# Layer 1 edges: a PSUM bank of VectorE's own for node numbers, group weights, directions and kv factors, and two banks of node sums

## The chip, the cores and the metric

The kernel runs on one core of a Trainium2 chip. A core has five engines, each with a queue of its own: TensorE (PE, matrix products, with the weight loads shown apart as PEld), VectorE (DVE), ScalarE (ACT), GpSimd (POOL) and SyncE (SP, which here only issues DMAs). Two memories lie on the core: SBUF, and PSUM with eight banks of 512 float32 a partition, into which TensorE writes its products. [...] The metric is the time of one execution on the device in microseconds (us), as the median of several runs.

## What is computed

The reference is a graph network of two layers on 3125 nodes with 256 features and 50,000 edges sorted by their target node. What matters here is the first part of layer 1: an attention over edges (`gnn`) and a linear attention over all nodes (`mix`), both on the normed nodes:

```python
# gnn: 64 features a message, 4 heads
h_fwd = h @ W_forward.T
h_rev = h @ W_reverse.T
messages = h_fwd[src] * direction[:, 0:1] + h_rev[src] * direction[:, 1:2]
scores = leaky_relu(einsum('ef,hf->eh', messages, attn_forward[0]), 0.2)
exp_scores = exp(scores - scores.max(axis=0))
sum_exp = segment_sum(exp_scores, dst, N)
norm = exp_scores / (sum_exp[dst] + 1e-10)
out[:, hd] = segment_sum(messages * norm[:, hd:hd + 1], dst, N)      # for each head

# mix: 8 heads of 64
q, k, v = heads of einsum('bnc,fc->bnf', x, Wqkv)
k, v = inst_norm(k), inst_norm(v)
out = einsum('bhnd,bhde->bhne', q, einsum('bhnd,bhne->bhde', k, v)) / n
out = einsum('bnf,cf->bnc', heads joined, Wout) + bout
```

After it follows a feed-forward part with four experts and a second edge attention that picks the experts.

## The kernel before

`layer1_mix` (L1530) does both parts in one loop. The 50,000 edges are laid out as 391 columns of 128, and `SPANS` cuts the columns into 50 groups: one of 4, 48 of 8, one of 3. For each group:

- `fetch` (L1562) issues one row gather for each column on POOL's queue (`gather`, L69): 128 rows of 136 numbers from the table `tab1` in DRAM, picked by a column of `t_src`, into a tile `g1` of which four exist. The gathers of three groups are issued ahead, and those of group i+3 in turn i of the loop.
- `messages` (L1569) makes the group's messages on VectorE. L1573 and L1575 multiply the two halves of the gathered rows by the edge's two directions `t_dir`, L1577 adds them, L1579 forms the scores, L1584 their maximum on each partition. TensorE turns that maximum (L1586).
- `weigh` (L1623), for the group before, multiplies the messages by the four exponents (L1624, 128x2048).
- `maximum` (L1589) keeps the running maximum of all scores: L1593 to L1595 on VectorE, with two more small transposes (L1599) on TensorE.
- `products` (L1627), for the group before, sums the weighted messages by node: matrix products (L1630) of the weighted messages with a matrix of zeros and ones, into a PSUM tile `pw`, of which three exist, a bank each.
- `add` (L1634), for two groups back, adds the sums into `acc`: L1638 and L1639 on VectorE, L1642 and L1640 on ScalarE.
- `ones_of` (L1612) makes the matrix of zeros and ones for the group: L1617 compares each edge's target `t_dst` with the node numbers of the group's window. The numbers lie in `turned` for even groups and in the first 128 columns of `self.node` for odd ones.
- `exponents` (L1602) subtracts the maximum (L1605) and lets ScalarE take the exponents (L1607) straight into the last column of the tile `v`.

A generator, `galerkin` (L1683), runs the linear attention in between: one step of it after most turns of the loop. In the steps for the 25 node tiles, VectorE sums the squares of keys and values (L1712), and multiplies the values by one factor a head (`kv_both`, L1713 to L1718), while TensorE makes keys and values (L274, from `token_matmul`) and their products (L1721). The last seven steps multiply out the result (L1776, L1778) and add it to `x` (L1769).

The loop stands under a manual schedule: TensorE, VectorE and ScalarE do their instructions in the order in which the program writes them. POOL does the gathers in its own order, SP the loads of weights. The PSUM is shared out in full: two banks for `ln_pt` (L1537), one for `pdots`, three for `pw` (L1539), two for `psm`.

Of the kernel before, what the change touches and what calls it, by code (L numbers as in the profile page):

```python
# [9 lines left out]
F32 = mybir.dt.float32  # L10
# [7 lines left out]
PSUM = bass.MemoryType.PSUM  # L18
# [4 lines left out]
P = 128  # L23
# [7 lines left out]
GROUP = 8  # L31
# [63 lines left out]
def held(t):  # L95

    return P if t < NT - 1 else REST
# [31 lines left out]
class Kernel:  # L129
# [1400 lines left out]
    def layer1_mix(self, acc):  # L1530
        nc, tc, a = self.nc, self.tc, self.a
        W, HD = 68, 64
        with ExitStack() as m:
            big = m.enter_context(tc.tile_pool(name="l1", bufs=1))
            wk = m.enter_context(tc.tile_pool(name="l1w", bufs=2))
            gp = m.enter_context(tc.tile_pool(name="l1g", bufs=3))
            ps_a = m.enter_context(tc.tile_pool(name="l1pa", bufs=2, space=PSUM))  # L1537
            ps_c = m.enter_context(tc.tile_pool(name="l1pc", bufs=1, space=PSUM))
            ps_w = m.enter_context(tc.tile_pool(name="l1pw", bufs=3, space=PSUM))  # L1539
            ps_s = m.enter_context(tc.tile_pool(name="l1ps", bufs=2, space=PSUM))  # L1540

            xT, tab1 = self.xT, self.tab1
# [5 lines left out]
            turned = big.tile([128, P], F32, name="turned")  # L1548
            for s, base in ((slice(0, HALF), HALF), (slice(HALF, P), 0)):
                nc.gpsimd.iota(turned[:, s], pattern=[[1, HALF]], base=base, channel_multiplier=0,  # L1550
                               allow_small_or_imprecise_dtypes=True)


            unit = big.tile([P, NT, 4], F32, name="unit")
            top = big.tile([4, 1], F32, name="top0")
# [6 lines left out]
            def fetch(i):  # L1562
                j0, n = SPANS[i]
                g = gp.tile([128, GROUP, 2 * W], F32, name="g1", bufs=4)
                for k in range(n):
                    gather(nc, g[:, k, :], tab1[:], self.t_src[:, j0 + k:j0 + k + 1])
                return g

            def messages(i, g):  # L1569

                j0, n = SPANS[i]
                o = gp.tile([128, GROUP, W], F32, name="msg1")
                nc.vector.tensor_mul(o[:, :n, :], g[:, :n, :W],  # L1573
                                     self.t_dir[:, j0:j0 + n, 0:1].to_broadcast([128, n, W]))
                nc.vector.tensor_mul(g[:, :n, W:], g[:, :n, W:],  # L1575
                                     self.t_dir[:, j0:j0 + n, 1:2].to_broadcast([128, n, W]))
                nc.vector.tensor_add(o[:, :n, :], o[:, :n, :], g[:, :n, W:])  # L1577
                s = gp.tile([128, GROUP, 4], F32, name="score1")
                nc.vector.scalar_tensor_tensor(s[:, :n, :], o[:, :n, HD:], 0.2, o[:, :n, HD:],  # L1579
                                               op0=OP.mult, op1=OP.max)  # L1580
                if j0 + n == NJ:
                    nc.vector.tensor_scalar(s[:, n - 1, :], s[:, n - 1, :], late, None, op0=OP.add)
                mx = gp.tile([128, 4], F32, name="mx1")
                nc.vector.tensor_reduce(mx, s[:, :n, :].rearrange("p j h -> p h j"), AX.X, OP.max)  # L1584
                pt = ps_s.tile([4, 128], F32, name="psm")
                nc.tensor.transpose(pt, mx, self.ident)  # L1586
                return o, s, pt

            def maximum(pt):  # L1589

                nonlocal top
                two = gp.tile([4, 3], F32, name="top")
                nc.vector.tensor_reduce(two[:, 2:3], pt, AX.X, OP.max)  # L1593
                nc.vector.tensor_tensor(two[:, 0:1], two[:, 2:3], top, OP.max)
                nc.vector.tensor_sub(two[:, 1:2], top, two[:, 0:1])  # L1595
                top = two[:, 0:1]
                pb = ps_s.tile([128, 2, 4], F32, name="psm")
                for i in range(2):
                    nc.tensor.transpose(pb[:, i, :], two[:, i:i + 1].to_broadcast([4, 128]), self.ident[:4, :4])  # L1599
                return pb  # L1600
# [11 lines left out]
            def ones_of(i):  # L1612

                j0, n = SPANS[i]
                hot = gp.tile([128, GROUP, P], F32, name="hot")
                iota = turned if i % 2 == 0 else self.node[:, :P]
                nc.vector.scalar_tensor_tensor(  # L1617
                    hot[:, :n, :], self.t_dst[:, j0:j0 + n, None].to_broadcast([128, n, P]),
                    float(HALF * (1 - i)), iota[:, None, :].to_broadcast([128, n, P]),
                    op0=OP.add, op1=OP.is_equal)  # L1620
                return hot

            def weigh(n, o, v):  # L1623
                nc.vector.tensor_mul(v[:, :n, :, :HD], o[:, :n, None, :HD].to_broadcast([128, n, 4, HD]),  # L1624
                                     v[:, :n, :, HD:].to_broadcast([128, n, 4, HD]))

            def products(n, v, hot):  # L1627
                pw = ps_w.tile([P, 4, HD + 1], F32, name="pw")
# [15 lines left out]
                    nc.scalar.copy(unit[p, t, :], big2[p, 0, :])  # L1644

            with tc.manual_schedule(engines={ET.PE, ET.DVE, ET.Activation}):
                todo = self.galerkin(big, wk, ps_a, ps_c, xT)
                S = len(SPANS)
                ahead = [fetch(i) for i in range(3)]
                msg, exps, summed = {}, {}, {}  # L1650
                for i in range(S + 2):
                    if i + 3 < S:
                        ahead.append(fetch(i + 3))
                    if i < S:
                        n = SPANS[i][1]
                        o, s, pt = messages(i, ahead[i])
                    if 0 <= i - 1 < S:
                        weigh(SPANS[i - 1][1], msg[i - 1][0], exps[i - 1][2])
                    if i < S:
                        pb = maximum(pt)  # L1660
                    if 0 <= i - 1 < S:
                        summed[i - 1] = products(SPANS[i - 1][1], exps[i - 1][2], msg[i - 1][1])
                    if 0 <= i - 2 < S:
                        add(i - 2, *exps[i - 2][:2], summed[i - 2])
                    if i < S:
                        msg[i] = o, ones_of(i)
                        exps[i] = exponents(n, s, pb)
                    if i % 4 != 3 or i > 34:
                        next(todo, None)
                last = exps[S - 1][0]  # L1670
                for _ in todo:
                    pass
# [7 lines left out]
            nc.vector.reciprocal(den, den)  # L1680
            nc.vector.tensor_mul(den, den, unit)

    def galerkin(self, big, wk, ps_a, ps_c, xT):  # L1683

        nc, a = self.nc, self.a
# [20 lines left out]
        for t in range(NT + 1):  # L1708
            if t > 0:
                kv, sq = kvs.pop(t - 1)  # L1710
                var = wk.tile([P, 16], F32, name="kv_var")
                nc.vector.tensor_reduce(var, sq, AX.X, OP.add)  # L1712
                nc.vector.tensor_scalar(var, var, 1.0 / 64, LN_EPS, op0=OP.mult, op1=OP.add)  # L1713
                both = wk.tile([P, 8], F32, name="kv_both")
                nc.vector.tensor_mul(both, var[:, 0:8], var[:, 8:16])
                nc.scalar.activation(both, both, AF.Sqrt)
                nc.vector.reciprocal(both, both)
                nc.vector.tensor_mul(kv[:, 8:, :], kv[:, 8:, :], both[:, :, None].to_broadcast([P, 8, 64]))  # L1718
                for hp in range(4):
                    p = held(t - 1)  # L1720
                    nc.tensor.matmul(pc[:, hp, :],  # L1721
                                     kv[:p, 8 + 2 * hp:10 + 2 * hp, :].rearrange("p a b -> p (a b)"),
                                     kv[:p, 2 * hp:2 * hp + 2, :].rearrange("p a b -> p (a b)"),
                                     start=(t == 1 and hp == 0), stop=(t == NT and hp == 3),
                                     skip_group_check=True)
            if t < NT:
                kv = wk.tile([P, 16, 64], F32, name="kv")
                for i in range(2):
                    pk = ps_a.tile([P, 512], F32, name="ln_pt")
                    self.token_matmul(pk, xT, t, wkv[:, :, 512 * i:512 * i + 512])  # L1730
                    nc.scalar.copy(kv[:, 8 * i:8 * i + 8, :].rearrange("p a b -> p (a b)"), pk)
                sq = wk.tile([P, 16, 64], F32, name="kv_sq", bufs=1)
                nc.scalar.activation(sq, kv, AF.Square)
                kvs[t] = kv, sq
            yield
# [22 lines left out]
        g = big.tile([128, 2, D], F32, name="gm")  # L1758
# [8 lines left out]
        for t0 in range(0, NT + 4, 4):  # L1767
# [3 lines left out]
            for t in range(t0, min(NT, t0 + 4), 2):  # L1771
                m = min(2, NT - t)
# [701 lines left out]
```

## Time and profile before

| | |
|---|---|
| median of 9 runs | 2994.75 us (2976.45 to 3017.75) |
| the profiled execution | 2987.9 us, span 2986.2 us |
| busy in the span: PE, DVE, ACT, POOL | 2138.5, 1468.0, 823.3, 1641.4 us |
| gathers of layer 1's edges (L69, into `g1`), first start to last start | 1739.4 to 2328.0 us |
| first and last L1573 (messages) start | 1746.3 and 2334.7 us |
| in 1800 to 1900 us: PE, DVE, ACT, POOL busy | 69.67, 75.29, 39.38, 79.89 us |
| in 2200 to 2330 us: PE, DVE, ACT, POOL busy | 104.97, 85.08, 11.23, 103.61 us |
| L1624, 128x2048, x50 | 112.5 us, mean 2249 ns |
| L1617, 128x1024, x25 with `turned`, x25 with `node` | 30.1 and 29.6 us, mean 1205 and 1183 ns |
| L1573, L1575, L1577, x50 each | 35.6, 35.2, 35.6 us |
| L1718, 128x512, x25 | 17.3 us, mean 692 ns |

The table is read so: the profile is of one execution, taken by the hardware, with the start and the duration of each instruction. "Busy" counts the time in which an engine works on an instruction, so a share well below the whole can still belong to the engine that sets the pace, if the rest of its time are gaps that belong to its work. In lists of groups, "idle before" is the time that the engine stood still just before these instructions, with what ended it; "issue" means that nothing in the profile was waited for. A gather's row is the time in which POOL handles it, not the transfer, which lands later.

### The profile page before, as it was taken

Reading aid. Unit: us, or ns where it says so; the run is one execution under the profiler, and the core shown is the slowest. Engines: PE = TensorE matmul, PEld = TensorE weight load, DVE = VectorE, ACT = ScalarE, POOL = GpSimd, SP = SyncE. Lnnn points to the kernel's source line nnn. Section 1 sums busy time; section 2 is a strip of 40 time slices with the busy share of each in tenths; the row PEclk is TensorE's granted clock in tenths of the full one; section 3 lists DMA queues with packets and bytes.
Section 4 is the critical chain, followed back from the end, with each engine's and each line's share of the span. In section 5 each row is a group of like instructions: output and inputs, shape, how many; then the busy total and the mean of one; then the engine's idle time right before and its main releaser. Section 6 shows DMA issues by size and latency. Waiting matters only on the chain.

```text
span 2986.2 us, 26612 instructions
## 1 busy us (share of the span) xinstructions
PE 2138.5 (72%) x8219; PEld 1479.8 (50%) x8219; DVE 1468.0 (49%) x3847; ACT 823.3 (28%) x1789; POOL 1641.4 (55%) x1931
## 2 busy tenths in 40 slices
PE   1455688278989699898999456676777566877935
PEld 0233344134555377787778334444455444545623
DVE  7258947366733493111111447777766711112345
ACT  1143133325522112223223223333410321212213
POOL 5858867680000803666664057787887376666220
PEclk9677699589968899999999678888888687988967
DMA  8312438021100214555554322222222111112123
GB/s 274 131 46 92 155 141 289 1 78 49 61 1 28 98 55 128 171 165 177 160 180 152 104 68 47 47 46 46 46 53 46 31 33 14 16 25 59 46 76 90
DMA packets 191716, 263.27 MB, mean 88 GB/s; under 512 B 57234, under 2 KB 152071, under 8 KB 191563
## 3 DMA queue, kind: packets, MB, share of 16 engines
q1 hardware_dynamic: 137551, 211.02, 21.4%
q0 software_dynamic: 48864, 45.64, 7.3%
q10 hardware_dynamic: 5148, 4.80, 0.5%
q8 instruction: 67, 1.10, 0.2%
q14 instruction: 86, 0.70, 0.1%
HBM read 180.80 MB, written 80.55 MB: 88 GB/s over the span
## 4 chain that ended last, share of the span: by engine, by line
PE 37%; issue 18%; DVE 14%; POOL 13%; another core or an unknown queue 9%; ACT 5%; DMA 3%; SPq 0%; ACTq 0%; DVEq 0%; POOLq 0%
POOL g L69 11%; PE pb L1138 6%; PE fph L1853 6%; PE fpy L1869 5%; PE pb L573 4%; PE pc L1147 4%; PE pb L274 2%; PE pc L573 2%; PE pc L956 2%; PE pb L616 1%; POOL adj L76 1%; PE pb L943 1%; DVE s_z L1362 1%; PE pc L1378 1%
## 5 line engine op out<-in xcount | busy, mean ns | idle before, releaser
L69 POOL DMA_INDIRECT g<-tab,t_src x391 | 471.1, 1205 | 201.4 <-issue 199.3
L76 POOL DMA_INDIRECT adj<-ch_sum,ch_place x391 | 408.3, 1044 | 174.1 <-issue 64.3
L76 POOL DMA_INDIRECT sorted<-src,pos x256 | 245.1, 958 | 170.4 <-DVE pos L1401 92.5
L69 POOL DMA_INDIRECT G<-tabg,g_src x256 | 250.9, 980 | 131.3 <-issue 73.0
L1138 PE MATMUL pb<-xs,w 128*128 128x256 f32 x1024 | 246.4, 397 | 42.8 <-ACT h L1140 41.3
L1853 PE MATMUL fph<-xT,fw 128*128 128x512 f32 (+2 forms) x448 | 193.1, 580 | 69.3 <-ACT fh L1855 41.0
L1138 PEld LDWEIGHTS pb<-xs,w 128*128 128x128 f32 x1024 | 201.1, 199 | 83.0 <-ACT h L1140 50.6
L1630 PE MATMUL pw<-v,hot 128*128 128x260 f32 x782 | 231.9, 461 | 0.0
L1147 PE MATMUL pc<-w,h 128*128 128x256 f32 x1024 | 226.1, 379 | 0.0
L1869 PE MATMUL fpy<-fw,fh 128*128 128x256 f32 (+1 forms) x800 | 185.5, 390 | 33.4 <-issue 33.2
L573 PE MATMUL pb<-adj,sup 128*128 128x448 f32 (+1 forms) x484 | 196.8, 552 | 15.6 <-DVE r_tot L1249 13.9
L1147 PEld LDWEIGHTS pc<-w,h 128*128 128x128 f32 x1024 | 192.2, 190 | 24.9
L1140 ACT ACTIVATE h<-pb,b 128x256 f32<-128x256 f32 x256 | 116.1, 473 | 316.4 <-issue 244.3
L1630 PEld LDWEIGHTS pw<-v,hot 128*128 128x128 f32 x782 | 177.4, 233 | 35.0
L1869 PEld LDWEIGHTS fpy<-fw,fh 128*128 128x128 f32 (+1 forms) x800 | 154.8, 195 | 69.5 <-issue 44.5
L1360 ACT ACTIVATE s_z<-s_y,s_val 128x128 f16<-128x128 f16 x256 | 112.4, 486 | 199.4 <-issue 190.4
L1853 PEld LDWEIGHTS fph<-xT,fw 128*128 128x128 f32 x448 | 89.1, 203 | 155.1 <-issue 86.4
L1855 ACT ACTIVATE fh<-fph,cols 128x512 f32<-128x512 f32 (+2 forms) x112 | 68.9, 632 | 344.4 <-remote 167.1
L1150 DVE SCALAR_TENSOR_TENSOR yo<-pc,own,bg 128x256 f32<-128x256 f32 x64 | 29.0, 481 | 235.0 <-PE pb L1138 170.7
L76 POOL DMA_INDIRECT slots<-rows,abi x50 | 52.3, 1047 | 164.3 <-DVE which L1061 154.7
L573 PEld LDWEIGHTS pb<-adj,sup 128*128 128x128 f32 x484 | 90.5, 194 | 93.0 <-issue 86.5
L76 POOL DMA_INDIRECT y<-yo,toi x64 | 61.4, 959 | 132.2 <-DVE yo L1150 119.0
(570 smaller groups left out, 3808.5 us busy)
## 6 DMA issues: line engine op xcount, KB each, us to landing
adj<-zero SPq DMA_DIRECT2D x25, 1600.0 KB
w<-in_L_ffn_W1p_dram SPq DMA_DIRECT2D x32, 1024.0 KB
w<-in_L_ffn_W2p_dram SPq DMA_DIRECT2D x32, 1024.0 KB
adj<-adj SPq DMA_DIRECT2D x24, 896.0 KB
adj<-adj SPq DMA_DIRECT2D x24, 704.0 KB
slots<-empty SPq DMA_DIRECT2D x1, 8448.0 KB
srow<-slots SPq DMA_DIRECT2D x32, 264.0 KB
adj<-ch_sum,ch_place POOLq DMA_INDIRECT x391
```

Source lines behind the costliest of these rows:

```text
L69: return nc.gpsimd.indirect_dma_start(out=out, out_offset=None, in_=table, in_offset=bass.IndirectOffsetOnAxis(ap=idx, axis=0))
L76: return nc.gpsimd.indirect_dma_start(out=table, out_offset=bass.IndirectOffsetOnAxis(ap=idx, axis=0), in_=rows, in_offset=None, **kw)
L274: self.nc.tensor.matmul(out, xT[:, k, t * P:(t + 1) * P], w[:, k, :], start=(k == 0), stop=(k == 1))
L573: nc.tensor.matmul(pm[:, :w], sup[:, b, k * 128:(k + 1) * 128], mats[b, h][:, c0 - PARTS[h][0]:c0 - PARTS[h][0] + w], start=(b == b0), sto ...
L1138: nc.tensor.matmul(ph, w1[:, k, f * 128:(f + 1) * 128], xs[:, k, :], start=(k == 0), stop=(k == 1))
L1140: nc.scalar.activation(h[:, f, :], ph, AF.Gelu, bias=b1[:, f:f + 1])
L1147: nc.tensor.matmul(py, h[:, f, i * 128:(i + 1) * 128], w2[:, f, :], start=(f == 0), stop=(f == FC - 1))
L1360: nc.scalar.activation(z[:, i, k, :], y, AF.Relu, bias=val[:, k, s], scale=val[:, 2 + k, s])
L1630: nc.tensor.matmul(pw.rearrange("p h c -> p (h c)"), hot[:, k, :], v[:, k, :, :].rearrange("p h c -> p (h c)"), start=(k == 0), stop=(k == ...
L1853: nc.tensor.matmul(ph[:, :m], w1[:, k, f * 128:(f + 1) * 128], xT[:, k, t0 * P:t0 * P + m], start=(k == 0), stop=(k == 1))
L1855: nc.scalar.activation(hs[:, f, :m], ph[:, :m], AF.Gelu, bias=self.col("L1_ffn_b1", ei * FC + f))
L1869: nc.tensor.matmul(py[:p], hs[:, f, i * P:i * P + p], w2[:, f, :], start=(f == 0), stop=(f == FC - 1))
```

## The change

One of the three banks of `pw` becomes a bank of VectorE's own, `own` (128x512). Before the loop, VectorE copies the two rows of node numbers into its first 256 columns. Three small areas behind them hold a group's weights (`weight`, 8 columns of edges x 4 heads), a group's directions (`sides`, 8 x 2), and the eight factors of the values (`scales`). In each turn VectorE copies the group's directions from `t_dir` into `sides` ahead of L1573, and the exponents from the last column of `v` into `weight` ahead of L1624; these two instructions and L1575 then take their second operand from the bank. L1617 takes the node numbers from there, and the reciprocal L1717 writes its result there, from where L1718 reads it. What is computed stays the same.

```diff
-            ps_w = m.enter_context(tc.tile_pool(name="l1pw", bufs=3, space=PSUM))
+            ps_w = m.enter_context(tc.tile_pool(name="l1pw", bufs=2, space=PSUM))
+            ps_d = m.enter_context(tc.tile_pool(name="l1pd", bufs=1, space=PSUM))
...
+            own = ps_d.tile([128, 512], F32, name="own_bank")
+            nc.vector.tensor_copy(own[:, 0:P], turned)
+            nc.vector.tensor_copy(own[:, P:2 * P], self.node[:, :P])
+            weight = own[:, 2 * P:2 * P + 4 * GROUP].rearrange("p (j h) -> p j h", h=4)
+            sides = own[:, 2 * P + 64:2 * P + 64 + 2 * GROUP].rearrange("p (j i) -> p j i", i=2)
...
-                nc.vector.tensor_mul(o[:, :n, :], g[:, :n, :W],
-                                     self.t_dir[:, j0:j0 + n, 0:1].to_broadcast([128, n, W]))
-                nc.vector.tensor_mul(g[:, :n, W:], g[:, :n, W:],
-                                     self.t_dir[:, j0:j0 + n, 1:2].to_broadcast([128, n, W]))
+                nc.vector.tensor_copy(sides[:, :n, :], self.t_dir[:, j0:j0 + n, :])
+                nc.vector.tensor_mul(o[:, :n, :], g[:, :n, :W], sides[:, :n, 0:1].to_broadcast([128, n, W]))
+                nc.vector.tensor_mul(g[:, :n, W:], g[:, :n, W:], sides[:, :n, 1:2].to_broadcast([128, n, W]))
...
-                iota = turned if i % 2 == 0 else self.node[:, :P]
+                iota = own[:, i % 2 * P:i % 2 * P + P]
...
             def weigh(n, o, v):
+                nc.vector.tensor_copy(weight[:, :n, :], v[:, :n, :, HD])
                 nc.vector.tensor_mul(v[:, :n, :, :HD], o[:, :n, None, :HD].to_broadcast([128, n, 4, HD]),
-                                     v[:, :n, :, HD:].to_broadcast([128, n, 4, HD]))
+                                     weight[:, :n, :, None].to_broadcast([128, n, 4, HD]))
...
-                todo = self.galerkin(big, wk, ps_a, ps_c, xT)
+                todo = self.galerkin(big, wk, ps_a, ps_c, xT, own[:, 2 * P + 96:2 * P + 104])
...
-    def galerkin(self, big, wk, ps_a, ps_c, xT):
+    def galerkin(self, big, wk, ps_a, ps_c, xT, scales=None):
...
-                nc.vector.reciprocal(both, both)
-                nc.vector.tensor_mul(kv[:, 8:, :], kv[:, 8:, :], both[:, :, None].to_broadcast([P, 8, 64]))
+                inverse = both if scales is None else scales
+                nc.vector.reciprocal(inverse, both)
+                nc.vector.tensor_mul(kv[:, 8:, :], kv[:, 8:, :], inverse[:, :, None].to_broadcast([P, 8, 64]))
```

## The prediction

> **What bounds the kernel now.** I read the chain of waits first, then the costliest groups, then the answer for the gather's line, and last the order of time inside the stage. The chain's dearest single line and the dearest group are the same one, the row gather of the layer 1 edges:
>
> ```profile
> POOL g L69 11%; PE pb L1138 6%; PE fph L1853 6%; PE fpy L1869 5%; PE pb L573 4%; PE pc L1147 4%; PE pb L274 2%; PE pc L573 2%; PE pc L956 2%; PE pb L616 1%; POOL adj L76 1%; PE pb L943 1%; DVE s_z L1362 1%; PE pc L1378 1%
> L69 POOL DMA_INDIRECT g<-tab,t_src x391 | 471.1, 1205 | 201.4 <-issue 199.3
> ```
>
> The gather's own answer gives its spread and who waits for it:
>
> ```profile
> L69 POOL DMA_INDIRECT g<-tab,t_src x391: 940/945/3025, 1739.4 to 2328.0; - x196
> ...
>   DVE msg L1573: 92.7, 36
> ```
>
> The median is 945 ns but the mean is 1205: a quarter of a microsecond too much, 391 times. Gaps between gathers are 0.30 us throughout (119 us summed over the stage), so an undisturbed gather costs 0.945 + 0.30 = 1.25 us and 391 of them 489 us. The stretch lasts 1739.4 to 2329.4, 590 us. The 101 us between are 153 gathers of 1 us or more (the other 238 are undisturbed). The order of time shows what stretches them (start, duration, engine):
>
> ```profile
> 2008.33 0.69 DVE L1718 TENSOR_TENSOR kv<-kv,kv_both 128x512 f32<-128x512 f32 x1
> ...
> 2010.74 0.73 DVE L1573 TENSOR_TENSOR msg<-g,t_dir 128x544 f32<-128x544 f32 x1 [1.72 <-DMA g<-tab,t_src]
> 2011.38 0.72 DVE L1575 TENSOR_TENSOR g<-g,t_dir 128x544 f32<-128x544 f32 x1
> 2011.57 1.35 POOL L69 DMA_INDIRECT g<-tab,t_src  x1 [0.30 <-issue]
> ...
> 2013.25 2.30 DVE L1624 TENSOR_TENSOR v<-msg,v 128x2048 f32<-128x2048 f32 x1
> 2013.57 0.27 PE L1586 MATMUL psm<-ident,mx 128*4 128x128 f32 x1
> 2014.47 1.89 POOL L69 DMA_INDIRECT g<-tab,t_src  x1 [0.30 <-issue]
> 2015.47 0.27 DVE L1593 TENSOR_REDUCE top<-psm 4x1 f32<-4x128 f32 x1
> ...
> 2016.60 0.43 DVE L1639 TENSOR_TENSOR acc<-acc,pw 64x260 f32<-64x260 f32 x1
> 2016.67 0.94 POOL L69 DMA_INDIRECT g<-tab,t_src  x1 [0.30 <-issue]
> 2017.06 1.22 DVE L1617 SCALAR_TENSOR_TENSOR hot<-t_dst,turned 128x1024 f32<-128x1024 f32 x1
> 2017.92 1.18 POOL L69 DMA_INDIRECT g<-tab,t_src  x1 [0.30 <-issue]
> ```
>
> Each long gather ends 0.81 to 0.83 us after a VectorE instruction: 2016.36 after 2015.55 (L1624), 2012.92 after 2012.10 (L1575), 2019.10 after 2018.28 (L1617). Sorted so, the 101 us belong to L1624 46.4, L1617 30.6, L1575 with L1573 17.4, L1718 3.6, one L1703 2.1, L1577 0.9, L1638 0.8. All of these read two operands from SBUF. None ends at L1639, L1769 (one operand in PSUM) or L1712 (one operand). The close pair is L1638 and L1639, equal in size: seven gathers that start 0.02 to 0.27 us into L1638 are all held to its end. Of 32 that start so into L1639, 17 run free, like the one at 2016.67 (0.94); the other 15 are held, but to the end of L1617, which follows closely.
>
> VectorE is the second limit. From the first L1573 (1746.3) to the last (2334.7) it takes 588.4 us, of which 82.6 are waits for gathers (92.9 in the stage, less 10.35 at the first). Its own pace, with its waits for TensorE and ScalarE, is 505.8 us, above the 489 of free gathers. So the stage can fall at most about 83 us, and what the change adds to VectorE comes off that.
>
> **The change, part by part.** *Taken off the gathers.* L1573, L1575, L1617, L1624 and L1718 each get one operand in PSUM. By the sort this frees 46.4 + 30.6 + 17.4 + 3.6 = 98 us of stall. L1577, L1638 and a few small ones stay; shifted against the gathers they may catch more than their 1.7 us. A gather every 1.25 us that starts at random in 0.72 (L1577) or 0.41 (L1638) loses 0.72²/2/1.25 + 0.41²/2/1.25 = 0.27 us a group, 13 us in 49. Gathers then need 489 + 13 = 502 us, still under VectorE's pace, so this is covered.
>
> [...]
>
> *Added to VectorE.* Two copies a group: `sides` (128x16) and `weight` (128x32).
>
> ```profile
> L1713 DVE TENSOR_SCALAR kv_var<-kv_var x25: 174/174/176, 1779.4 to 2165.2; 128x16 f32<-128x16 f32 x25
> ...
> L1639 DVE TENSOR_TENSOR acc<-acc,pw x49: 416/419/429, 1786.9 to 2344.8; 64x260 f32<-64x260 f32 x49
> ...
> L1638 DVE TENSOR_TENSOR acc<-acc,grown x49: 409/422/428, 1786.5 to 2344.3; 64x260 f32<-64x260 f32 x49
> ```
>
> An instruction that doesn't need its predecessor starts 0.08 before that one's end (L1573 to L1575), one that does starts 0.04 after it (L1577 to L1579). So `sides` costs 0.17 + 0.04 = 0.21 and `weight` 0.19 (as L1579 and L1605, 32 elements) + 0.04 = 0.23. No row shows VectorE writing PSUM or reading back what it just wrote there. Low end: nothing, where VectorE waits anyway. High end: each as L1638, 0.42 + 0.12 = 0.54. Nearest in size are the 16 and 32 element rows; I take 0.27 each, 0.54 a group, the excess for the unseen PSUM write. In seven groups (36 and 38 to 43) VectorE waits 2.8 to 8.1 us for TensorE at L1593 or L1754 and the copies vanish there; 42 of the 49 periods pay: 42 x 0.54 = 22.7 us (low 0, high 42 x 1.08 = 45).
>
> *A PSUM operand in place of an SBUF one.* L1639 against L1638: 419 and 422 ns. L1769 reads 128x512 from PSUM in 672 ns, L1718 takes 691 from SBUF. I take 0. That a word is read again and again by a broadcast from PSUM is in no row; its upper price is the slower rival.
> [...]
>
> *Costs of nothing, with their cover.* The reciprocal L1717 only writes elsewhere. The two copies that fill the bank (0.30 each, as L1216's 128x136 copy) fall before the first message, where VectorE idles 10.35 us; uncovered, 0.6. `weight` waits for the exponent of the group before (L1607), done some 6 us earlier; only at the last group, where L1624 waits 0.29 now, does it stand behind it. With two banks of sums, L1630 waits for ScalarE's copy L1642 of two groups back, a period old (7 us or more). No DMA and nothing on SP's or POOL's queue moves; POOL's gathers will wait for a free `g1` buffer, that is for L1577 four groups back, some 20 us in all, which costs nothing because VectorE is then the bound.
>
> *Where the stall goes.* When VectorE no longer waits for gathers, TensorE could be late for L1593: after L1718 ends (2009.02) it needs to 2013.84, 4.8 us; VectorE needs 4.65 + 0.54 = 5.2 over the same stretch. Just covered.
>
> **Sum.** Stage 588.4 becomes 505.8 + 22.7 = 528.5, 60 us less. Everything after hangs on the stage's end. The profiled execution took 2987.9 (span 2986.2), so 2928 for it; the median of the runs is 2994.75, 6.9 above, and 2994.75 - 60 gives **2935**. Own range: copies at nothing, 2912; copies at 0.54, 2957.
>
> **Rivals.**
> *Lengthened copies.* Each write into PSUM and read back costs as much as 0.54 or somewhat more: 505.8 + 45 to 60, gain 23 to 38, time 2957 to 2972. For it: no row of such a pair. Against it: every tiny VectorE row is under 0.25. Chance 0.12.
> *The hold isn't removed.* A gather stalls for these ops wherever their second operand lies. Then the gathers still set 590 us, the copies hide in the 82.6 us of waits, and the time stays at 2995, within 5. For it: L1617 and L1624 are longer than any PSUM row here. Against it: the 17 free gathers in L1639. Chance 0.05.
> *Slower: repeated PSUM reads at half rate.* If a broadcast operand from PSUM took two cycles an element, L1624, L1617, L1573, L1575 and half an L1718 would add 2.13 + 1.07 + 0.57 + 0.57 + 0.27 = 4.6 us a group, 42 x 4.6 = 193, and the stage would be 505.8 + 22.7 + 193 = 721, 133 longer: 3128. It decides from 60/42 = 1.4 us a group, that is a third slower. For it: contiguous reads are all that the rows show. Against it: SBUF broadcasts run at full rate (L1624, 2.30 us for 2048). Chance 0.11.
>
> **How the numbers follow.** Forecast 0.72, the three rivals 0.12, 0.05 and 0.11. A measurement tells about 0.5% (15 us) from no change. Faster takes the forecast and the first rival, 0.84; the second is the same, 0.05; slower 0.11. The runs before spread by 0.7% either way, so I widen the own range by 4 below and take in most of the first rival above: 2908 to 2968.
>
> **What would show it.** The gather's mean falls from 1205 to below 1000 ns, with no long one ending 0.82 after L1624, L1617, L1575 or L1718; L1573's wait for gathers falls from 92.7 to under 20 us; POOL begins to wait for L1577; L1624 stays at 2.30 and L1617 at 1.2; the new copies read 0.17 to 0.30. A longer L1624, or a gather mean still above 1150, would prove me wrong.

## The result and the profile after

The changed kernel takes 3060.2 us (median of 20 runs, 3016.9 to 3076.5) against 2992.6 for the kernel before (62 runs): ratio 1.020, interval 1.017 to 1.023. It is about 2% slower, where 2935 was forecast. Its profiled span is 3037.0 us. Every ratio here is of fast executions alone, those within 1.5% of the fastest of their kernel, so it can differ from the quotient of the medians of all (1.023 here), and the traces of e4 and e6 below are of executions just outside that bound.

The page of the changed kernel, with the chain of waits by engine and by line, and the row of the gathers:

```profile
PE 41%; DVE 21%; another core or an unknown queue 15%; issue 14%; ACT 6%; DMA 2%; POOL 1%; ACTq 0%; DVEq 0%; SPq 0%; POOLq 0%
PE pb L1138 7%; PE pb L573 6%; PE fph L1859 5%; PE fpy L1875 5%; PE pc L1147 4%; DVE v L1629 2%; PE pc L573 2%; PE pc L956 2%; PE pb L274 1%; PE pc L1378 1%; PE pb L616 1%; ACT L1721 1%; DVE hot L1621 1%; PE pb L943 1%
...
L69 POOL DMA_INDIRECT g<-tab,t_src x391 | 372.2, 952 | 355.2 <-issue 202.1
```

The gather's mean fell from 1205 to 952 ns, and its line has left the chain. The holds are gone, as forecast. But the stage from the first message to the last (now L1579, 1724.8 to 2389.9) takes 665.1 us instead of 588.4. The chain has 15% of "another core or an unknown queue", although the program runs on one core: that share is time in which an engine waited for a semaphore and no instruction in the profile ended when it rose. The list of waits of the changed kernel (total, times, longest) says who waited so; "remote" is the same thing there:

```profile
ACT kv L1737 <- remote: 173.8, 11, 19.9
POOL g L69 <- DVE score L1583: 148.7, 21, 13.8
...
DVE top L1597 <- remote: 104.3, 11, 13.5
```

VectorE's row for L1597 shows 155.1 us idle in front of it, 104.3 of "remote" and 29.1 of "issue" among it. 665.1 less these two is 531.7, and 528.5 was forecast: these stalls account for the whole loss. The order of time shows one of them (start, duration, engine):

```profile
2030.80 3.17 PE L274 MATMUL ln_pt<-wkv,xT 128*128 128x512 f32 x7
...
2031.33 2.29 DVE L1629 TENSOR_TENSOR v<-msg,own_bank 128x2048 f32<-128x2048 f32 x1
...
2033.80 0.27 PE L1590 MATMUL psm<-ident,mx 128*4 128x128 f32 x1
2034.56 0.94 POOL L69 DMA_INDIRECT g<-tab,t_src  x1 [0.30 <-issue]
...
2040.80 0.94 POOL L69 DMA_INDIRECT g<-tab,t_src  x1 [0.30 <-issue]
2045.65 1.07 ACT L1737 COPY kv<-ln_pt 128x512 f32<-128x512 f32 x2 [18.46 <-remote]
2045.75 0.28 DVE L1597 TENSOR_REDUCE top<-psm 4x1 f32<-4x128 f32 x1 [12.13 <-remote]
```

TensorE is done with L1590 at 2034.07. ScalarE and VectorE go on only at 2045.65 and 2045.75. The trace also records when each semaphore rises: those of the two halves of L274 (ended 2032.25 and 2033.96) and of L1590 rose at 2045.63, 2045.69 and 2045.72. Elsewhere such a rise follows the end of its product by 0.01 to 0.02 us. By these ends the products are there, and their completion signals come 11.7 to 13.4 us late. (The end of a matrix product is modelled in the profile, so a late signal can't be told there from a product that is itself finished late.) All the while GpSimd issues gathers one each 1.25 us, until all four `g1` buffers are full; the signals come 4 us after its last gather ends. In the stage 66 signals are late by over 0.3 us, by 414 us in sum (they overlap); in the kernel before 6 are, by 19 us. None of VectorE's signals on record there is late.

The prices of the new operands (groups of VectorE in the stage of the changed kernel):

```profile
L1629 DVE TENSOR_TENSOR v<-msg,own_bank 128x2048 f32<-128x2048 f32 (+2 forms) x50 | 111.9, 2239 | 1.7
L1621 DVE SCALAR_TENSOR_TENSOR hot<-t_dst,own_bank 128x1024 f32<-128x1024 f32 (+2 forms) x50 | 59.4, 1188 | 0.7
...
L1628 DVE COPY own_bank<-v 128x32 f32<-128x32 f32 (+2 forms) x50 | 10.3, 206 | 0.3 <-ACT v L1611 0.3
...
L1578 DVE COPY own_bank<-t_dir 128x16 f32<-128x16 f32 (+2 forms) x50 | 8.7, 175 | 0.9
```

Broadcast reads from PSUM cost here what they cost from SBUF in before (2239 against 2249 ns in the mean of all 50, 2287 against 2297 for the 48 of 128x2048), so the slower rival of the prediction, half the rate, is not what happened.

### The profile page after: what moved, and what is told of

It reads as the page before. It is cut to its first block, busy times and chain, and to the rows that moved or that the text cites. A ratio compares the mean times of both kernels' runs of the same rounds, so it can differ in the third digit from the quotient of the medians.

```text
span 3037.0 us, 26715 instructions
## 1 busy us (share of the span) xinstructions
PE 2146.4 (71%) x8219; PEld 1487.8 (49%) x8219; DVE 1484.3 (49%) x3949; ACT 822.9 (27%) x1789; POOL 1544.6 (51%) x1931
## 4 chain that ended last, share of the span: by engine, by line
PE 41%; DVE 21%; another core or an unknown queue 15%; issue 14%; ACT 6%; DMA 2%; POOL 1%; ACTq 0%; DVEq 0%; SPq 0%; POOLq 0%
PE pb L1138 7%; PE pb L573 6%; PE fph L1859 5%; PE fpy L1875 5%; PE pc L1147 4%; DVE v L1629 2%; PE pc L573 2%; PE pc L956 2%; PE pb L274 1%; PE pc L1378 1%; PE pb L616 1%; ACT L1721 1%; DVE hot L1621 1%; PE pb L943 1%
## 5 line engine op out<-in xcount | busy, mean ns | idle before, releaser
L69 POOL DMA_INDIRECT g<-tab,t_src x391 | 372.2, 952 | 355.2 <-issue 202.1
L1635 PE MATMUL pw<-v,hot 128*128 128x260 f32 x782 | 239.0, 472 | 0.0
L1603 PE MATMUL psm<-ident,top 4*128 4x4 f32 x100 | 16.5, 220 | 200.7 <-ACT kv L1737 103.5
```

The lines of the kernel that those rows point to most:

```text
L69: return nc.gpsimd.indirect_dma_start(out=out, out_offset=None, in_=table, in_offset=bass.IndirectOffsetOnAxis(ap=idx, axis=0))
L1635: nc.tensor.matmul(pw.rearrange("p h c -> p (h c)"), hot[:, k, :], v[:, k, :, :].rearrange("p h c -> p (h c)"), start=(k == 0), stop=(k == ...
```

## The experiments

Each set ran on one chip with its own runs of the kernel before. One thing must be known to read them: in the first two sets the kernel before took 3036 and 3044 us, in the last three 2605, 2606 and 2605. "Late" counts TensorE signals over 0.3 us late in the stage, and their sum. Where records of signals are missing, each recorded one is given to a product that had ended by then, in order, so that the sum is the least possible.

| set, run | edit | ratio to before [95%] | stage, us | late |
|---|---|---|---|---|
| before | | | 588.4 | 6, 19 us |
| after | | 1.020 [1.017, 1.023] | 665.1 | 66, 414 us |
| 1 e1_spaced | after, a memset behind each gather | 1.033 [1.022, 1.044] | 670.4 | 57, 446 us |
| 1 e2_two_banks | before, two banks of sums | 1.012 [1.000, 1.023] | 589.6 | 10, 5 us |
| 1 e3_bank_not_read | after, SBUF operands | 1.008 [1.003, 1.013] | 603.0 | 11, 93 us |
| 1 e4_before_spaced | before, a memset behind each gather | 1.022 [1.009, 1.035] | 660.1 | none |
| 2 e5_shifted | after, 62 transposes ahead | 1.016 [1.010, 1.021] | 642.7 | 56, 332 us |
| 2 e6_pause | after, four memsets a group | 1.012 [1.003, 1.021] | 636.3 | 69, 340 us |
| 2 e7_weights_sbuf | after, L1629 on SBUF | 1.007 [1.001, 1.013] | 623.5 | 57, 270 us |
| 2 e8_half_pause | after, two memsets a group | 1.023 [1.016, 1.031] | 663.5 | 61, 403 us |
| 3 e9_two_memsets | after, two memsets behind each gather | 1.021 [1.020, 1.023] | 640.6 | none |
| 3 e10_half_gathers | after, half the gathers, the other rows zero | 0.975 [0.973, 0.977] | 519.4 | none |
| 3 e11_numbers_only | before, node numbers alone in the bank, two banks of sums | 0.988 [0.986, 0.990] | 557.6 | none |
| 3 e12_experts | before, smaller burst for the experts | 1.000 [0.999, 1.002] | 591.4 | none |
| 4 e13_after_again | after | 0.975 [0.974, 0.977] | 523.3 | none |
| 4 e14_numbers_again | as e11 | 0.988 [0.986, 0.989] | 555.8 | none |
| 4 e15_numbers_weights | after, directions in SBUF | 0.976 [0.974, 0.978] | 523.5 | none |
| 5 e16, e17, e18 | as e11, e10, e9 | 0.988, 0.975, 1.021 | 557.0, 520.3, 640.5 | none |

**Set 1: stream, banks, or traffic in the bank.** The theory was that gathers in an unbroken stream hold up TensorE's signals, and that VectorE's holds had been the breaks in it.

```diff
-                    gather(nc, g[:, k, :], tab1[:], self.t_src[:, j0 + k:j0 + k + 1])
+                    self.spaced(gather(nc, g[:, k, :], tab1[:], self.t_src[:, j0 + k:j0 + k + 1]))
```

> After, with one GpSimd memset of 128x128 behind every layer 1 gather, the same that the kernel already puts behind its scatters. Theory A (TensorE's completion signals come late while GpSimd issues gathers back to back, one each 1.25 us; the VectorE holds had been the breaks): the seven stalls of 11 to 13 us and the long ones of the first groups go, the stage falls from about 665 to 530-545 us, time 2930 to 2950. Theories B (two banks of sums make TensorE late) and C (VectorE's traffic in its PSUM bank holds TensorE up): the stalls stay, time 3050 to 3090, since gathers only get slower.

The stalls stayed. Order of time of this kernel:

```profile
2052.66 0.27 PE L1590 MATMUL psm<-ident,mx 128*4 128x128 f32 x1
...
2062.34 0.95 POOL L69 DMA_INDIRECT g<-tab,t_src  x1 [0.16 <-issue]
2063.29 0.22 POOL L291 MEMSET idle<- 128x128 f32 x1
2066.07 1.07 ACT L1737 COPY kv<-ln_pt 128x512 f32<-128x512 f32 x2 [19.09 <-remote]
2066.17 0.28 DVE L1597 TENSOR_REDUCE top<-psm 4x1 f32<-4x128 f32 x1 [12.76 <-remote]
```

The reader sees the same picture with a memset between gathers: a spacer of 0.22 us is no break. The same edit to the kernel before:

> Before, with the memset behind every gather. It separates the spacer's own price from its cure: A: before's one 8 us stall in the stage goes, but GpSimd is the stage's pace there and gets longer by 391 x about 0.1 us less what hides under holds: 2990 to 3035. If the spacer makes a kernel faster by itself, whatever else it does, this one falls below 2980 as well.

This made it slower too, 1.022: the spacer has a price (stage 660.1 us). Before's one stall of 8 us is not there, but one stall is too little to call that a cure. Two banks:

```diff
-            ps_w = m.enter_context(tc.tile_pool(name="l1pw", bufs=3, space=PSUM))
+            ps_w = m.enter_context(tc.tile_pool(name="l1pw", bufs=2, space=PSUM))
```

> Before, with only the banks of node sums cut from three to two. Theory B: TensorE waits for a free bank, time well above before, towards 3060. A and C: no change, 2990 to 2997, ratio 0.998 to 1.002, no new wait at the first product of a group.

The stage is 589.6 against 588.4, so giving up the third bank costs nothing there; the 1.012 of the whole isn't found in the stage, and its interval begins at 1.000. Then the bank written but not read by the large instructions:

```diff
-                nc.vector.tensor_mul(o[:, :n, :], g[:, :n, :W], sides[:, :n, 0:1].to_broadcast([128, n, W]))
+                nc.vector.tensor_mul(o[:, :n, :], g[:, :n, :W], self.t_dir[:, j0:j0 + n, 0:1].to_broadcast([128, n, W]))
...
-                iota = own[:, i % 2 * P:i % 2 * P + P]
+                iota = turned if i % 2 == 0 else self.node[:, :P]
...
-                                     weight[:, :n, :, None].to_broadcast([128, n, 4, HD]))
+                                     v[:, :n, :, HD:].to_broadcast([128, n, 4, HD]))
```

> After, with the bank still there and every copy into it still made (a second reciprocal makes the kv factors for SBUF), but the five large VectorE instructions read SBUF operands as in before. Theory A: gathers are held again, mean near 1205 ns, no regular stalls of 11 to 13 us, time 2990 to 3000 (the copies hide in the waits for gathers). C in the form that writes into the bank disturb TensorE: slow like after, near 3060. B: near 3060.

The gathers are held again (mean 1190 ns) and the regular stalls are gone; 11 late signals are left, up to 20.5 us, ten of them between 2222 and 2273 us, where most gathers run free. The whole is 1.008, a little more than expected. So neither two banks nor writes into the bank bring the regular stalls. This run takes away the reads of the bank and the free gathers together, so it doesn't tell these two apart. Against the reads speak its own late signals and those of before: no large instruction reads the bank there.

**Set 2: place or break.** A rival theory was that TensorE's fetch of instructions (16 KB about every 250 of its records: after's page has 67 packets and 1.10 MB on the queue q8, "instruction", and 16,438 records of PE and PEld; it starts some 1.6 us after five of the seven regular stalls of after) waits for a gap in the gathers. 62 transposes ahead of the loop move the fetches to other groups:

```diff
+                pt = ps_s.tile([4, 128], F32, name="psm")
+                for _ in range(62):
+                    nc.tensor.transpose(pt[:, :4], self.ident[:4, :4], self.ident[:4, :4])
```

> After, with 62 small transposes (62 weight loads, 62 products) on TensorE ahead of the first group, where TensorE stands idle. Theory D: TensorE must fetch 16 KB of instructions about every 250 records, and cannot while gathers follow each other without a gap of some 1.5 us in their packets (0.7 us in after). Then the same stalls of 11 to 13 us move: after 124 more instructions they come two groups earlier (about 7, 11, 15, 19, 23, 27, 31 in place of 9, 13, 17, 21, 25, 29, 33), and the time stays within 1% of after, 3050 to 3080 on a chip where before takes 2993. Rival P (a fixed point of the program, such as the turn without a step of the linear attention, makes TensorE late): the stalls stay in groups 9, 13, 17 and so on.

Neither happened. The long waits mostly came at the turn without a step of the linear attention, one group earlier than in after, with signals 5 to 12 us late. There the fetch is long over: 2024.7, while the signal of L1590 is late afterwards.

```profile
2028.75 0.27 PE L1590 MATMUL psm<-ident,mx 128*4 128x128 f32 x1 [1.02 <-DVE mx L1588]
...
2034.34 0.95 POOL L69 DMA_INDIRECT g<-tab,t_src  x1 [0.30 <-issue]
2034.93 0.28 DVE L1597 TENSOR_REDUCE top<-psm 4x1 f32<-4x128 f32 x1 [3.79 <-remote]
```

This signal comes with the gathers still running, so they need not stop for it. The fetch is not what is waited for. Three kernels then tried breaks of different kinds: four memsets behind each group's last gather, two, and one held gather a group (L1629 back on SBUF, its copy gone).

```diff
-                    gather(nc, g[:, k, :], tab1[:], self.t_src[:, j0 + k:j0 + k + 1])
+                    ins = gather(nc, g[:, k, :], tab1[:], self.t_src[:, j0 + k:j0 + k + 1])
...
+                for _ in range(4):
+                    self.spaced_after(ins)
                 return g
```

> After, with four GpSimd memsets of 128x128 in a row behind the last gather of each group (about 0.9 us), none between the gathers of a group. Theory D with the gap: a gap of about 1.6 us in the packets once a group lets the fetch through; the stalls of 11 to 13 us go, gathers take 489 + 50 x 0.9 = 534 us, the stage about 535 to 545, ratio to before 0.980 to 0.988. If a gap of this size is too small: stalls stay, ratio 1.02 to 1.03.

> As the run with four memsets a group, with two (about 0.45 us; gap in the packets about 1.15 us). It places the threshold: if 1.15 us is enough, gathers take 489 + 23 = 512, VectorE's 528 is the bound, ratio 0.975 to 0.982; if not, stalls stay at fetches and the ratio is 1.01 to 1.03.

```diff
-                nc.vector.tensor_copy(weight[:, :n, :], v[:, :n, :, HD])
                 nc.vector.tensor_mul(v[:, :n, :, :HD], o[:, :n, None, :HD].to_broadcast([128, n, 4, HD]),
-                                     weight[:, :n, :, None].to_broadcast([128, n, 4, HD]))
+                                     v[:, :n, :, HD:].to_broadcast([128, n, 4, HD]))
```

> After, with one of the five instructions given back its SBUF operand: the products with the weights read the exponents where ScalarE put them, and the copy of the weights goes. Theory D with the gap: this instruction (2.3 us) holds one gather a group to its end, a gap of 1.6 us or more; the fetches pass there, the stalls go; gathers 489 + 46 of hold + some 10 for collisions = 545, the stage 540 to 550, ratio to before 0.983 to 0.990. Rival C (VectorE's other reads of its bank disturb TensorE): stalls stay, ratio above 1.01.

All three missed: 57 to 69 late signals each, with a sum of 340 us for four memsets, 403 for two and 270 for the held gather, against 414. One break a group is not enough; the three holds or so that a group has in before mostly are (e3, e4).

**Set 3: rate or holds.** Two memsets behind every gather, half the gathers (half of the messages are left out), the node numbers alone in the bank, and the same question in another stage.

```diff
+                    if k % 2:
+                        nc.gpsimd.memset(g[:, k, :], 0.0)
+                        continue
                     gather(nc, g[:, k, :], tab1[:], self.t_src[:, j0 + k:j0 + k + 1])
```

```diff
-FIRST, SHARE, BEHIND_BY = 24, 3.05, 3
+FIRST, SHARE, BEHIND_BY = 8, 3.3, 3
```

> After, with two memsets of 128x128 behind every gather instead of one: a gather each 1.58 us, nothing held. Theory R (what counts is the mean rate over some tens of us: at one gather each 1.25 to 1.33 us a backlog builds up behind which TensorE's signals wait, at before's mean of 1.5 us it does not): signals late by over 0.3 us fall from some 60 in the stage to under 15, the regular stalls go; the gathers then take 391 x 1.58 = 618 us, the stage about 620, ratio to before 1.008 to 1.016, faster than the run with one memset. Theory H (it takes a VectorE instruction that holds GpSimd to let signals through): the signals stay late, stage above 660, ratio above 1.03.

> After, with every second column's gather left out and its part of the tile set to zero by a GpSimd memset; the rest is computed as before on those columns. Theories R and H both: about 4 gathers a group, no stream, no late signals, no gather waits; the stage then shows VectorE's own pace with the bank, which the forecast put at 528 us: ratio to before 0.975 to 0.985. Rival C (VectorE's traffic in its bank makes TensorE late): stalls stay, ratio above 1.0.

> Before, with the bank and two banks of sums, but only the node numbers in it (no copies in the loop; the other four instructions read SBUF). It takes away the hold of one instruction a group (30.6 us of 101) and leaves the holds of the 2.3 us product and of the two direction products. If rate decides (R, limit near 1.5 us a gather): the freed time comes back as late signals, stage 585 to 600, ratio 0.997 to 1.005. If some holds a group are enough (H): stage about 489 + 70 = 560, ratio 0.988 to 0.993.

> Before, unchanged in layer 1; in the feed-forward part the first burst of gathers is cut from 24 to 8 and the later share raised from 3.05 to 3.3 for each finished tile. There TensorE stands still for 33 us while some 50 gathers run at 1.25 us, and no instruction of that part uses VectorE's bank. If a stream of gathers makes TensorE late by itself (A, R): that idle stretch shrinks to under 15 us, time 5 to 25 us less, ratio 0.992 to 0.998, unless the graph attention behind it comes to wait. If TensorE waits there for something else: the stretch stays, ratio 1.0.

The set could not answer what it was made for. Here the kernel before takes 2605 us, and no TensorE signal of the stage is late in any of the four: all 243 are on record, none over 0.05 us behind its product. The stretch of 33 us in the experts isn't there either, so the smaller burst moves nothing. The row of ScalarE's L1855 in the feed-forward part shows the difference of conditions best; before as profiled for the prediction, then e12, whose L1855 does the same work:

```profile
L1855 ACT ACTIVATE fh<-fph,cols 128x512 f32<-128x512 f32 (+2 forms) x112 | 68.9, 632 | 344.4 <-remote 167.1 <-PE fph L1853 133.0 <-issue 32.2
```

```profile
L1855 ACT ACTIVATE fh<-fph,cols 128x512 f32<-128x512 f32 (+2 forms) x112 | 70.1, 633 | 214.8 <-PE fph L1853 214.7
```

The work is equal (632 and 633 ns each); what is gone is "remote". Among the 200 dearest waits of before, 16 are of this kind, 580 us in sum (they overlap); the stage has one of them, of 8.1 us (total, times, longest):

```profile
ACT fh L1855 <- remote: 167.1, 16, 44.3
DVE s_hot L1351 <- remote: 59.2, 7, 20.5
...
DVE top L1593 <- remote: 8.1, 1, 8.1
```

e12's 200 have none. The stage of before takes as long under both conditions (588.4 and 591.4 us in e12, granted clock 0.85 and 0.84), so the 390 us between before's two times lie outside it. What the set did show is the gain without late signals: half the gathers give a stage of 519.4, and the node numbers alone 557.6 against e12's 591.4, 34 us for the 30.6 of holds that the sort gave to that instruction. The two memsets came out as priced for most gathers (one each 1.59 us in the median, 1.58 expected), but the mean is 1.65, and the stage 640.6 instead of 620.

**Set 4: the change itself again.**

> The changed kernel once more, unaltered. In the last four runs before took 2605 us instead of some 3000, and in none of the four was a TensorE signal in this stage late by over 0.3 us, with or without a stream of gathers. Theory M (the late signals are a condition of the chip that a run falls on, and the change pays only there): where before takes about 2605, after has no regular stall, a stage of 526 to 535 us (VectorE's pace, as forecast) and a ratio of 0.975 to 0.981; where before takes about 3000, the stalls of 11 to 13 us are there and the ratio is 1.01 to 1.03. Rival N (the change itself makes TensorE late, wherever it runs): stalls and a ratio above 1.005 also where before takes 2605.

> The run with the node numbers alone in the bank, once more. Where before takes about 2605: as then, stage 567 us, ratio 0.986 to 0.990. Where before takes about 3000: the gathers lose one hold of three a group; theory M with the freed stream as trigger: more late signals than before's 12 but fewer than the 55 to 68 of the freed kernels, ratio 0.99 to 1.01.

```diff
-                nc.vector.tensor_copy(sides[:, :n, :], self.t_dir[:, j0:j0 + n, :])
-                nc.vector.tensor_mul(o[:, :n, :], g[:, :n, :W], sides[:, :n, 0:1].to_broadcast([128, n, W]))
+                nc.vector.tensor_mul(o[:, :n, :], g[:, :n, :W], self.t_dir[:, j0:j0 + n, 0:1].to_broadcast([128, n, W]))
```

> After, with the directions read from SBUF again and their copy left out: it saves VectorE 0.2 us a group and gives the gathers back the 17.4 us of holds at the two direction products. Where before takes about 2605: VectorE's pace 505.8 + some 10 = 516, gathers 489 + 17.4 + 10 to 13 = 517 to 520, stage 517 to 530, ratio 0.972 to 0.979, the fastest of the three. Where before takes about 3000: late signals, ratio 1.00 to 1.02.

The unaltered changed kernel took 2540.4 us against 2605.7: ratio 0.975 [0.974, 0.977]. From its page, then from its list of waits:

```profile
PE 48%; DVE 20%; POOL 14%; DMA 7%; issue 6%; ACT 3%; ACTq 0%; DVEq 0%; SPq 0%; POOLq 0%
...
L69 POOL DMA_INDIRECT g<-tab,t_src x391 | 377.4, 965 | 210.7 <-issue 195.1
```

```profile
DVE top L1597 <- PE psm L1590: 25.0, 12, 9.3
```

The chain has no "another core" share, L1597 waits 25.0 us for TensorE itself instead of 133, and the stage takes 523.3 us. The same code under two conditions shows what the late signals cost: with signals on time the change gains 65 us, with late ones it loses 68. Of the 142 us between the two stages, 130 are the idle time ahead of L1597 (155.1 and 25.0). The granted clock of the stage differs too, 0.82 against 0.91, but TensorE is busy for only 24 us less (391.1 instead of 414.8). e15 gained no more: VectorE saves a copy a group, but waits 44.1 us for TensorE at its L1596 instead of 25.0, so TensorE is the next bound.

**Set 5**, for the conditions of the first sets; they did not come again, and the results of sets 3 and 4 repeated.

> Node numbers alone in the bank, a third time, in the hope of a chip on which before takes about 3000 us and TensorE's signals come late. There: gathers keep two holds a group; if these are enough the stage is about 565 as where nothing is late, ratio 0.990 to 0.995; if late signals take it back, ratio 0.998 to 1.01. Where before takes about 2605: ratio 0.986 to 0.990 again.

> After with every second column's gather left out (its part of the tile set to zero), once more. Where before takes about 3000: if late signals need a dense stream of gathers, none here, stage 526 as on the other chip, ratio about 0.980; if any gather at 1.25 us does it or the change itself does, late signals and stalls remain, ratio above 0.99. Where before takes about 2605: 0.973 to 0.977 again.

> After with two memsets behind every gather (one each 1.58 us, none held), once more. Where before takes about 3000: theory R (rate) few late signals, stage about 650 from the memsets alone as on the other chip, ratio 1.018 to 1.024; theory H (only holds let signals through) late signals as in after on top, ratio above 1.035. Where before takes about 2605: 1.019 to 1.023 again.

What makes the signals late, and why in sets 1 and 2 and in the runs of the result but not in sets 3 to 5, stays open. The number of the chip doesn't tell: sets 1 and 4 both ran on chip 0. One rival that no run tests is the recording itself. Every time on record comes with a span from the profiler, and where signals are late the record has large holes: in after's stage 505 of VectorE's 823 signals are on record and 1419 landings of DMAs, in e13 all 823 and 6237. Whether the recording delays the signals, or both come from one cause, no run decides. It also stays open whether the gathers' rate or the holds decide there, and whether the node numbers alone would pay there: none of the kernels made for that ran with late signals. No version is known that beats before under both conditions; where nothing is late, the changed kernel, level with e15, is the fastest tried that computes everything.

## Why the prediction was wrong

- **The holds and their sort: right.** The gather's mean fell from 1205 to under 1000 ns in both conditions (952 and 965), and the part freed by the node numbers alone was 34 us for 30.6 forecast. With the five instructions' operands back in SBUF the mean is 1190 ns (e3), so here it is the move of one of two operands to PSUM that shortens the gathers.
- **The copies: right, a little high.** 0.175 and 0.206 us each in after; e13's stage of 523.3 is 17.5 over VectorE's 505.8, where 22.7 was taken.
- **PSUM operands at 0: right**, 2239 against 2249 ns and 1188 against the 1205 and 1183 of before. The slower rival's 4.6 us a group is an estimate, one more pass over its 4416 elements at before's 1.045 ns each (2297 less 725 ns, over 2048 less 544 elements, L1624 and L1577); the rows of after show none of it. **Two banks at nothing: right** for the stage (e2).
- **GpSimd waits for a free buffer: right in kind.** It waits for L1583, 148.7 us in after, but only because VectorE stands still there; in e13 the wait is 11.7 us.
- **The sum: right where signals are on time** (stage 68 us shorter than e12's, 65 us in the whole, 60 forecast), and wrong for the measured result.

The step that failed is "Where the stall goes": TensorE was found "just covered" at L1593, 4.8 us against 5.2. It compared the two engines' work and took for granted that a product is known to VectorE when it is done. In after, the signal of L1590 came 11.4 to 13.3 us after its product in the regular stalls, and 18.2 us once. No rival covered this: the one called "slower" had the direction, but by longer instructions, which did not come. Neither of the two signs that were named as proof against the forecast came, a longer L1624 or a gather mean above 1150. The trace of before held the sign that mattered. These are lines of before, from the order of time, at a place of the stage where six gathers ran free in a row:

```profile
2277.64 0.27 PE L1586 MATMUL psm<-ident,mx 128*4 128x128 f32 x1
...
2282.91 0.94 POOL L69 DMA_INDIRECT g<-tab,t_src  x1 [0.30 <-issue]
2283.65 0.28 DVE L1593 TENSOR_REDUCE top<-psm 4x1 f32<-4x128 f32 x1 [8.11 <-remote]
```

The prediction counted this 8.1 us among VectorE's waits "for TensorE". But TensorE's L1586 ended at 2277.91, 5.7 us before; the releaser reads "remote", not L1586. The chain of before had 9% of "another core or an unknown queue" on a program of one core, and in the experts TensorE stood still for 33 us (2436 to 2469) while gathers streamed at 1.25 us beside it:

```profile
PE 37%; issue 18%; DVE 14%; POOL 13%; another core or an unknown queue 9%; ACT 5%; DMA 3%; SPq 0%; ACTq 0%; DVEq 0%; POOLq 0%
```

```profile
2467.64 0.94 POOL L69 DMA_INDIRECT G<-tabg,g_src  x1 [0.30 <-issue]
...
2469.23 3.78 PE L1869 MATMUL fpy<-fw,fh 128*128 128x256 f32 x8 [33.16 <-issue]
```

Read so, the change turns the whole layer 1 stage into such a stretch, and under the condition of the result it pays for that.

## What to carry to other kernels

Before a stall is removed, look at how the other engines fare where it is already absent in the same trace: here the stretches with free gathers were the ones with unexplained waits. "Another core" or "remote" on a one-core program is a finding to be priced, not a remainder. And a wait that is put down to an engine should be checked against the end of that engine's instruction; if it ended long before, work isn't what is missing.

## What the runs showed of the hardware

- In sets 1 and 2 TensorE completion signals rose up to 37.5 us after their product by the profile's modelled end (e8, where VectorE's longest wait of "remote" is 36.8 us; 31.6 in e1, with a wait of 31.0), while none of the 505 VectorE signals on record in after's stage is late. In these profiles late signals go with gathers issued one each 1.25 us (after) to 1.33 us (e1), 56 to 69 of them in the stage (after, e1, e5 to e8); with the holds of before there are 6. In e13, with gathers one each 1.25 us as well, none is late. Where signals are late a part of the semaphore records is missing as well (29 of TensorE's 243 in after's stage, 37 in before's), in set 3 none.
- The condition matters more than the change: before itself took 2605 us or some 3000. VectorE's and ScalarE's instructions took the same time (L1624 2249 ns, and 2248 in e12), some of TensorE's after layer 1 up to 6% longer (L1853 580 ns, and 545 in e12).
